# Layer 0 of a four-layer conditional residual network: four batches at once, as 2x2 blocks with seven block products in place of eight

## The chip, the cores and the metric

The kernel runs on one core of a Trainium2 chip. The time is the device time of one launch in microseconds. A core has TensorE (PE; its weight loads are shown as PEld), VectorE (DVE), ScalarE (ACT), GpSimd (POOL) and SyncE (SP, which only issues DMAs here). Each runs its own instructions in the order in which they were written, and waits on semaphores for the others.

## The reference

Activations x are 8 batches x 256 tokens x 1024 features. Each layer adds to x:

```
x = x + L0(x): x @ W0.T + 2 * lora, where logits = x @ Wr.T + 5 * onehot(lang[b]),
        the two best of 8 experts are gated by a softmax of their logits,
        h = x @ A[e].T (16 ranks for each expert), lora = (h * gate) @ B[e].T
x = x + L1(x): x @ W1.T + b1 + coeff[b] * (x @ (2 * mask[b] - 1))
x = x + L2(x): x @ w2[ids[b]].T           (1024 x 1024 weights, chosen for each batch)
x = x + L3(x): (x @ B3[ids[b]]) @ A3[ids[b]]   (rank 16)
```

W0 is the same for all batches; the weights of layers 1 and 2 differ from batch to batch.

## The kernel before

**Precision.** Every large product is split: each operand becomes a high half (a cast to fp32r, by ACT) and a low half (the source less the high half, by DVE), and TensorE adds hi·hi, hi·lo and lo·hi in PSUM. `three` (lines 408-423) does it with three 512-column matmuls for each k-block, 24 in all. `two` (425-439) has hi and lo of x side by side, 256 columns each, and needs eight matmuls of 512 and eight of 256 columns. The residual x + x @ W.T is had by adding the identity to W's diagonal block (`add_identity`, line 159) before it is split.

**Order.** The kernel works on pairs of batches q = 0..3 (512 tokens), one pair after another. `units` (lines 109-117) lists the work for a pair: "A" (the experts' first product, 24 matmuls), eight units of layer 0 (one for each block m of 128 output features, 24 matmuls each and three for the low-rank term, `lora`, line 451), sixteen of layer 1 and sixteen of layer 2 (m and batch j of the pair, each `two`). Layer 3 has rank 16 and is spread between other units (`proj`, `rank`, `fill`). `slot(i)` (line 656) writes all engines' work for unit i by hand: load the weights nine units ahead (`load`, SP's queue), `evacuate` the unit before out of PSUM (ACT copies one half, DVE adds the other), make high halves four units ahead (`prep_hi`, line 184) and low halves three ahead (`prep_lo`, 191), and then the matmuls (`main`). Layer 1's weights of a batch, mask times coefficient plus W1, are merged six or seven units ahead: `merge` (154, ACT) and `merge_add` (174, DVE).

**Router.** `logits` (259), transposes to token order (270), then some twenty small DVE operations and one exponential on ACT (`router`, lines 273-318) for the pair; `gate` (320) multiplies the experts' product by the gates and splits it, for `lora`.

**Buffers.** Ten 512 KB tiles for raw weights, five for high and four for low halves of weights, four x tiles of 2 MB, PSUM as two groups of four banks.

**Start.** `first_products` (486) interleaves the splits of x, of the experts' weights and of the first unit with their matmuls in pieces of 256 columns, as the first DMAs land.

Of the kernel before, what the change touches and what calls it, by code (L numbers as in the profile page):

```python
# [8 lines left out]
F32 = mybir.dt.float32  # L9
# [6 lines left out]
P = 128  # L16
NB = 8
T = 256
K = 8
E = 8  # L20
R = 16
LOAD_AHEAD = 9
PREP_AHEAD = 4
MERGE_AHEAD = (6, 7)
W1_BUFS = 3
RAW_BUFS = 10
# [6 lines left out]
def kernel(ctx: ExitStack, tc: tile.TileContext, x, lang, coeff, ids,  # L33
# [3 lines left out]

    nc = tc.nc
# [4 lines left out]
    hlp = ctx.enter_context(tc.tile_pool(name="hl", bufs=4))  # L43
    xp = ctx.enter_context(tc.tile_pool(name="xp", bufs=2))
    rawp = ctx.enter_context(tc.tile_pool(name="raw", bufs=RAW_BUFS))
    wp = ctx.enter_context(tc.tile_pool(name="w", bufs=4))
    l3p = ctx.enter_context(tc.tile_pool(name="l3", bufs=4))
    gp = ctx.enter_context(tc.tile_pool(name="g", bufs=1))
    ps = ctx.enter_context(tc.tile_pool(name="ps", bufs=4, space=PS))
    aux = ctx.enter_context(tc.tile_pool(name="aux", bufs=4, space=PS))  # L50

    D = PREP_AHEAD
    f32 = lambda ap: ap.bitcast(F32)


    xraw = {}

    def load_x(b, h, parts=1):

        t = rawp.tile([P, K // 2, T], F32, tag="raw", name=f"x{b}_{h}")  # L60
        n = K // 2 // parts
        for i in range(parts):
            c = slice(i * n, (i + 1) * n)
            nc.sync.dma_start(t[:, c, :], x[b, :, h * K // 2 + i * n:h * K // 2 + (i + 1) * n, :])
        xraw[b, h] = t
# [13 lines left out]
    for g in range(1, 4):  # L79
        nc.vector.tensor_tensor(sel, sel, ident[:, 32 * g:32 * g + R], ALU.add)  # L80
# [6 lines left out]


    def split(hi, lo, src):
        nc.scalar.copy(hi, src)  # L90
        return lambda: nc.vector.tensor_tensor(lo, src, f32(hi), ALU.subtract)

    x0 = {}

    def split_x(q):
        x0[q] = tuple(hlp.tile([P, K, 2 * T], FR, tag="hl", name=f"x0{h}{q}")
                      for h in ("hi", "lo"))

    def split_x_part(q, j, h, k0=0, k1=K // 2):
        hi, lo = x0[q]  # L100
        c = slice(j * T, (j + 1) * T)
        src = xraw[2 * q + j, h][:, k0:k1, :]
        k = slice(h * K // 2 + k0, h * K // 2 + k1)
        nc.scalar.copy(hi[:, k, c], src)
        return lambda: nc.vector.tensor_tensor(lo[:, k, c], src, f32(hi[:, k, c]),
                                               ALU.subtract)


    units = []
    for q in range(NB // 2):  # L110
        units.append(("A", q, 0, 0))
        units += [("L0", q, m, 0) for m in range(K)]
        units += [("L1", q, m, j) for m in range(K) for j in range(2)]
        order = [(m, j) for m in range(K) for j in range(2)]
        if q == NB // 2 - 1:
            order[-6:] = [(m, j) for j in range(2) for m in range(K - 3, K)]
        units += [("L2", q, m, j) for m, j in order]
    raws, ws, w1raw = {}, {}, {}

    def parts(i):  # L120

        n = 2 if i < 2 else 1
        return [slice(j * K // n, (j + 1) * K // n) for j in range(n)]

    def load(i):
        if i >= len(units):
            return
        kind, q, m, j = units[i]
        b = 2 * q + j
        if kind == "L1":  # L130
            if j == 0:
                w = rawp.tile([P, K, P], F32, tag="w1", name=f"w1_{q}_{m}", bufs=W1_BUFS)
                nc.sync.dma_start(w, w1[m])
                w1raw[q, m] = w
            t = rawp.tile([P, K, P], I32, tag="raw", name=f"raw{i}")
            nc.sync.dma_start(t, mask[b, m])
        else:
            t = rawp.tile([P, K, P], F32, tag="raw", name=f"raw{i}")
            if kind == "A":
                for c in parts(i):  # L140
                    nc.sync.dma_start(t[:, c], la[:, c])
            elif kind == "L0":
                for c in parts(i):
                    nc.sync.dma_start(t[:, c], w0[m][:, c])
            else:
                src = w2[bass.ds(adapter(b), 1), m]
                nc.sync.dma_start(t, src.rearrange("a p k c -> (a p) k c"))
        raws[i] = t


    def merge(i):
        if i < len(units) and units[i][0] == "L1":
            b = 2 * units[i][1] + units[i][3]
            nc.scalar.activation(f32(raws[i]), raws[i], AF.Identity,  # L154
                                 bias=negc[:, b:b + 1], scale=c2[:, b:b + 1])

    def add_identity(w, m):

        nc.vector.tensor_tensor(w[:, m, :], w[:, m, :], ident, ALU.add)  # L159

    folded = set()

    def fold(i):
        if i < len(units) and units[i][0] in ("L0", "L2") and i not in folded:
            add_identity(raws[i], units[i][2])
            folded.add(i)

    def merge_add(i):
        if i < len(units) and units[i][0] == "L1":
            s = f32(raws[i])  # L170
            _, q, m, j = units[i]
            if j == 0:
                add_identity(w1raw[q, m], m)
            nc.vector.tensor_tensor(s, s, w1raw[q, m], ALU.add)  # L174

    def source(i):
        return f32(raws[i]) if units[i][0] == "L1" else raws[i]

    def prep_hi(i):
        if i < len(units):  # L180
            fold(i)
            hi = wp.tile([P, K, P], FR, tag="whi", name=f"whi{i}", bufs=D + 1)
            for c in parts(i):
                nc.scalar.copy(hi[:, c], source(i)[:, c])  # L184
            ws[i] = hi

    def prep_lo(i):
        if i < len(units):
            lo = wp.tile([P, K, P], FR, tag="wlo", name=f"wlo{i}", bufs=D)
            for c in parts(i):  # L190
                nc.vector.tensor_tensor(lo[:, c], source(i)[:, c], f32(ws[i])[:, c],  # L191
                                        ALU.subtract)
            ws[i] = (ws[i], lo)
            raws.pop(i)
# [9 lines left out]
    nc.sync.dma_start(wrs, wr)  # L204
    load_x(0, 0, 2)
    load(0)
    load_x(0, 1, 2)
    load(1)
    load_x(1, 0, 2)
    load_x(1, 1, 2)  # L210
    lang_i = cst.tile([P, NB], I32, name="lang_i")
    nc.sync.dma_start(lang_i, lang.rearrange("(a b) -> a b", a=1).to_broadcast([P, NB]))
    c_sb = cst.tile([P, NB], F32, name="c_sb")
    nc.sync.dma_start(c_sb, coeff.rearrange("(a b) -> a b", a=1).to_broadcast([P, NB]))
    ids_raw = cst.tile([1, NB], I32, name="ids_raw")
    nc.sync.dma_start(ids_raw, ids.rearrange("(a b) -> a b", a=1))
    b1_sb = cst.tile([P, K], F32, name="b1_sb")
    nc.sync.dma_start(b1_sb, b1)

    load(2)  # L220
    lb_raw = rawp.tile([P, K * P], F32, tag="raw", name="lb_raw")
    nc.sync.dma_start(lb_raw, lb)

    bias = cst.tile([P, NB, E], F32, name="bias")
    c2 = cst.tile([P, NB], F32, name="c2")
    negc = cst.tile([P, NB], F32, name="negc")
    ids_sb = cst.tile([1, NB], I32, name="ids_sb")
    lbs = [cst.tile([P, K * P], FR, name=f"lb{n}") for n in range(2)]

    def constants():  # L230

        lang_f = cst.tile([P, NB], F32, name="lang_f")
        nc.vector.tensor_scalar(lang_f, lang_i, -1.0, float(E), ALU.mult, ALU.add)
        nc.vector.tensor_tensor(bias, rev.to_broadcast([P, NB, E]),
                                lang_f.rearrange("p (b o) -> p b o", o=1)
                                      .to_broadcast([P, NB, E]), ALU.is_equal)
        nc.vector.tensor_scalar(bias, bias, 5.0, None, ALU.mult)
        nc.vector.tensor_scalar(c2, c_sb, 2.0, None, ALU.mult)
        nc.vector.tensor_scalar(negc, c_sb, -1.0, None, ALU.mult)

        neg = cst.tile([1, NB], F32, name="neg")
        idf = cst.tile([1, NB], F32, name="idf")
        nc.vector.tensor_scalar(neg, ids_raw, 0.0, float(E), ALU.is_lt, ALU.mult)
        nc.vector.tensor_tensor(idf, ids_raw, neg, ALU.add)
        nc.vector.tensor_scalar(ids_sb, idf, 0.0, float(E - 1), ALU.max, ALU.min)


    NT = 4

    pls = {}  # L250

    def logits(b, h):


        q, j = divmod(b, 2)
        if (j, h) == (0, 0):
            pls[q] = aux.tile([P, 512], F32, tag="aux", name=f"pl{q}")
        for g in range(4):
            nc.tensor.matmul(pls[q][32 * g:32 * g + 32, j * T:(j + 1) * T],  # L259
                             wrs[:, 4 * h + g, :], xraw[b, h][:, g, :],  # L260
                             start=(h == 0), stop=(h == 1))
# [555 lines left out]
```

## Time and profile before

| what | value |
|---|---|
| median of 3 runs | 626.79 us (626.68 to 627.22) |
| profiled execution | 626.69 us, span 624.9 us |
| mean granted TensorE clock | 0.997 of full |
| PE / PEld / DVE / ACT / POOL busy | 99 / 84 / 74 / 58 / 0% of the span |
| DMA | 125.01 MB, 200 GB/s over the span |

The span goes from the first to the last instruction; the time has some 1.8 us around it. In a view of groups, a row has the line, engine, operation, output and inputs, shape and count, then busy time and the mean of one in ns, then the engine's idle time ahead of such instructions and who ended it. In a timeline, a row begins with the start and the duration in us. Durations of instructions that follow each other on an engine overlap, so their pace is read from one start to the next. The rows of tenths cut the span into 40 equal slices.

### The profile page before, as it was taken

Reading aid. Unit: us, or ns where it says so; the run is one execution under the profiler, and the core shown is the slowest. Engines: PE = TensorE matmul, PEld = TensorE weight load, DVE = VectorE, ACT = ScalarE, POOL = GpSimd, SP = SyncE. Lnnn points to the kernel's source line nnn. Section 1 sums busy time; section 2 is a strip of 40 time slices with the busy share of each in tenths; the row PEclk is TensorE's granted clock in tenths of the full one; section 3 lists DMA queues with packets and bytes.
Section 4 is the critical chain, followed back from the end, with each engine's and each line's share of the span. In section 5 each row is a group of like instructions: output and inputs, shape, how many; then the busy total and the mean of one; then the engine's idle time right before and its main releaser. Section 6 shows DMA issues by size and latency. Waiting matters only on the chain.

```text
span 624.9 us, 9250 instructions
## 1 busy us (share of the span) xinstructions
PE 616.8 (99%) x3458; PEld 522.9 (84%) x3458; DVE 460.8 (74%) x800; ACT 363.0 (58%) x552; POOL 1.0 (0%) x14
## 2 busy tenths in 40 slices
PE   8999999999999999999999999999999999999996
PEld 6888888888788888888878888888888888888885
DVE  6685898776657799778656689967765678987642
ACT  5375797564354498656335558865535446975421
POOL 0000000000000000000000000000000000000000
PEclk9999999999999999999999999999999999999998
DMA  8964575667725775475942778547684458755004
GB/s 279 400 213 162 201 269 174 201 210 278 252 68 169 230 273 195 143 246 190 345 140 76 203 238 278 179 142 249 197 315 135 130 174 270 246 191 170 34 0 136
DMA packets 38815, 125.01 MB, mean 200 GB/s; under 512 B 4722, under 2 KB 5874, under 8 KB 38770
## 3 DMA queue, kind: packets, MB, share of 16 engines
q1 hardware_dynamic: 38626, 124.15, 59.8%
q8 instruction: 27, 0.44, 0.3%
q10 hardware_dynamic: 144, 0.26, 0.1%
q14 instruction: 18, 0.15, 0.1%
HBM read 116.01 MB, written 8.39 MB: 199 GB/s over the span
## 4 chain that ended last, share of the span: by engine, by line
PE 98%; DMA 1%; SPq 0%; DVE 0%; ACT 0%; DVEq 0%; issue 0%
PE po L428 37%; PE po L436 20%; PE po L412 9%; PE po L420 9%; PE po L413 9%; PE po L454 1%; PE po L455 1%; PE po L456 1%; PE pl L259 1%; PE po L388 1%; PE pb L468 1%; PE ph L413 1%; PE ph L412 1%; PE ph L420 1%; DMA raw<-in_la 1%; PE ph L497 0%
## 5 line engine op out<-in xcount | busy, mean ns | idle before, releaser
L428 PE MATMUL po<-hl,whi 128*128 128x512 f32 x1016 | 254.5, 392 | 0.0
L428 PEld LDWEIGHTS po<-hl,whi 128*128 128x128 f32 x1016 | 182.9, 189 | 32.9
L191 DVE TENSOR_TENSOR wlo<-raw,whi 128x1024 fp32r<-128x1024 f32 (+1 forms) x166 | 199.1, 1205 | 2.1 <-ACT whi L184 2.1
L184 ACT CAST whi<-raw 128x1024 fp32r<-128x1024 f32 (+1 forms) x166 | 172.4, 1039 | 10.6 <-DVE raw L159 7.9
L436 PEld LDWEIGHTS po<-hl,wlo 128*128 128x128 f32 x1016 | 137.9, 190 | 11.3 <-DVE raw L159 1.2
L436 PE MATMUL po<-hl,wlo 128*128 128x256 f32 x1016 | 142.4, 283 | 0.0
L412 PE MATMUL po<-x0hi,whi 128*128 128x512 f32 x248 | 97.1, 392 | 0.0
L413 PE MATMUL po<-x0lo,whi 128*128 128x512 f32 x248 | 96.7, 390 | 0.0
L174 DVE TENSOR_TENSOR raw<-raw,w 128x1024 f32<-128x1024 f32 x64 | 78.1, 1221 | 3.6 <-ACT raw L154 2.6
L154 ACT ACTIVATE raw<-raw,negc,c 128x1024 f32<-128x1024 int32 x64 | 79.7, 1245 | 0.0
L717 ACT COPY xt<-po 128x256 f32<-128x256 f32 x63 | 23.4, 372 | 83.6 <-PE po L436 83.6
L420 PE MATMUL po<-x0hi,wlo 128*128 128x512 f32 x248 | 62.3, 393 | 0.0
L710 ACT CAST hl<-po 128x256 fp32r<-128x256 f32 x64 | 20.5, 377 | 71.6 <-PE po L456 71.4
L726 DVE TENSOR_TENSOR xt<-po,xt 128x256 f32<-128x256 f32 x63 | 26.7, 423 | 47.0 <-ACT xt L717 46.7
L724 DVE TENSOR_TENSOR hl<-po,hl 128x256 fp32r<-128x256 f32 x64 | 23.8, 420 | 46.1 <-ACT hl L710 40.7
L412 PEld LDWEIGHTS po<-x0hi,whi 128*128 128x128 f32 x248 | 46.5, 188 | 11.1 <-issue 1.2
L413 PEld LDWEIGHTS po<-x0lo,whi 128*128 128x128 f32 x248 | 46.6, 188 | 9.8
L420 PEld LDWEIGHTS po<-x0hi,wlo 128*128 128x128 f32 x248 | 45.4, 188 | 8.8
L720 ACT ACTIVATE sum<-po,b_sb 128x256 f32<-128x256 f32 x64 | 30.4, 475 | 23.4 <-PE po L436 23.1
L726 DVE TENSOR_TENSOR sum<-po,sum 128x256 f32<-128x256 f32 x64 | 26.9, 420 | 12.7 <-ACT sum L720 12.6
L724 DVE TENSOR_TENSOR hl<-sum,hl 128x256 fp32r<-128x256 f32 x64 | 26.9, 420 | 4.6 <-ACT hl L710 4.6
L710 ACT CAST hl<-sum 128x256 fp32r<-128x256 f32 x64 | 25.6, 400 | 7.6 <-DVE sum L726 7.6
(118 smaller groups left out, 378.8 us busy)
## 6 DMA issues: line engine op xcount, KB each, us to landing
raw<-in_w SPq DMA_DIRECT2D x95, 512.0 KB, 4.2
raw<-in_mask SPq DMA_DIRECT2D x64, 512.0 KB, 5.2
w<-in_w SPq DMA_DIRECT2D x32, 512.0 KB, 4.8
out<-xt SPq DMA_DIRECT2D x31, 256.0 KB, 3.1
x<-in_x SPq DMA_DIRECT2D x12, 512.0 KB, 4.6
a3raw<-in_a SPq DMA_DIRECT2D x8, 384.0 KB, 3.6
x<-in_x SPq DMA_DIRECT2D x8, 256.0 KB, 5.4
raw<-in_la SPq DMA_DIRECT2D x3, 512.0 KB, 3.4
```

The source lines that it names most:

```text
L154: nc.scalar.activation(f32(raws[i]), raws[i], AF.Identity, bias=negc[:, b:b + 1], scale=c2[:, b:b + 1])
L174: nc.vector.tensor_tensor(s, s, w1raw[q, m], ALU.add)
L184: nc.scalar.copy(hi[:, c], source(i)[:, c])
L191: nc.vector.tensor_tensor(lo[:, c], source(i)[:, c], f32(ws[i])[:, c], ALU.subtract)
L412: nc.tensor.matmul(po, hi[:, k, :], xhi[:, k, :], start=(k == 0), stop=False)
L413: nc.tensor.matmul(po, hi[:, k, :], xlo[:, k, :], start=False, stop=False)
L420: nc.tensor.matmul(po, lo[:, k, :], xhi[:, k, :], start=False, stop=(last and k == K - 1))
L428: nc.tensor.matmul(po, hi[:, k, :], xhl[:, k].rearrange("p h t -> p (h t)"), start=(k == 0), stop=False)
L436: nc.tensor.matmul(po[:, :T], lo[:, k, :], xhl[:, k, 0, :], start=False, stop=(k == K - 1))
L710: nc.scalar.copy(hi, p)
L724: nc.vector.tensor_tensor(lo, p, f32(hi), ALU.subtract)
L726: nc.vector.tensor_tensor(xs, p[:, :T], xs, ALU.add)
```

## The change

Layer 0 is done for four batches (a group g, two pairs p0 = 2g and p1 = 2g+1) at once. W0 is cut into 2x2 blocks A11..A22 of 512 output by 512 input features; x is cut into 2x2 blocks B11..B22 of 512 input features by one pair's 512 tokens. The 2x2 product is had by seven block products with sums and differences (S1..S4 of A, T1..T4 of B) in place of eight. Each block product is two slots of 24 matmuls (half of the inner dimension each, over four output blocks). A slot has two items of 512 KB to split: one of A or S, one of B or T. A group has 16 slots for layer 0: 14 for products, and slots 4 and 5, which make only the second pair's experts' product (12 matmuls each); the first pair's is beside slots 0 to 3 (6 matmuls each). Layers 1 and 2 then follow for each pair as before.

What moves with it:

- DVE makes S2, S3, T1, T2 and T3 from the raw blocks, in place (ten 1024-wide differences for a group). S1, S4 and T4 are made by DMAs from POOL's queue that add to a block in SBUF (`accum_op`), six for a group. Four merges of layer 1 in each group are also done by such a DMA.
- The sums of products are built in SBUF: ACT copies C11 and U2 out of PSUM, DVE adds into U2, U3, C21, C22 and C12 (ten 1024-wide additions), and `split_c` splits each pair's C for layer 1.
- The identity is added to diagonal blocks by POOL, not by DVE (`fold_block`).
- PSUM tiles are pairs of banks, two such tiles in rotation and four single banks. In layers 1 and 2 the two batches of an output block share one and are evacuated by one instruction (`joint`).
- x, the sums C, the split x of layer 1 and of layer 2 live in three 4 MB regions that are used in turn. Raw weights have nine tiles in place of ten, W1 two in place of three.
- Group 0's second router runs in slot 7 of layer 0; group 1's two routers run together at the end of layer 2 of pair 1.
- At the start, SP loads x and W0's first blocks in k-blocks, and the small constants after them.

The diff, cut to what carries this:

```diff
+    L0_PRODUCTS = [("A11", "B11"), ("A12", "B21"), None, ("S2", "T2"), ("S3", "T3"),
+                   ("A22", "T4"), ("S1", "T1"), ("S4", "B22")]
...
+    def merge_add(n):
...
+        if by_dma(q, m):
+            fold_block(s[:, m, :])
+            nc.gpsimd.dma_start(s, w1[m], accum_op=ALU.add)
+            return
...
+    def prep_lo(n):
+        if n not in los:
+            los[n] = wp.tile([P, 1024], FR, tag="wlo", name=f"wlo{n}", bufs=LO_AHEAD + 1)
+        return los[n]
...
+    def product(s, g, kks, start=False, lora=None, mid=()):
...
+        for m in range(4):
+            o = mms[g][m // 2][:, m % 2, :]
...
+            if m == 2:
+                for f in mid:
+                    f()
+            if lora:
+                lora(m, o)
+            for k in kks:
+                link(o, w[0][:, k, c], v[0][:, k], start=(start and k == 0), stop=False)
+                link(o, w[0][:, k, c], v[1][:, k], start=False, stop=False)
+            for k in kks:
+                link(o, w[1][:, k, c], v[0][:, k], start=False, stop=(k == 1))
...
+        o = 1 if g == 0 else 0
+        at(0 + o, *subs("S3", "A11", "A21", 0, 1), folds)
+        if g == 0:
+            at(1, constants)
+            at(3, lambda: router([p0]), lambda: expand(p0), lb_parts)
+            at(-5, lambda: gate(p0))
+            at(7, lambda: router([p1]), lambda: expand(p1))
+            at(10, lambda: gate(p1))
+        else:
+            at(-5, lambda: gate(p0))
+            at(2, lambda: expand(p0))
+            at(7, lambda: expand(p1))
+            at(8, lambda: gate(p1))
+        at(1 + o, lambda: s1_add(0), lambda: s1_add(1), *subs("T1", "B12", "B11", 0, 1))
+        at(2 + o, *subs("S2", "S3", "A22", 0), *subs("T2", "T1", "B22", 0))
+        at(3 + o, *subs("S2", "S3", "A22", 1), *subs("T2", "T1", "B22", 1))
+        at(5, lambda: t4_add(0))
+        at(6, lambda: t4_add(1), *subs("T3", "B22", "B12", 0, 1))
+        at(7, lambda: s4_add(0), lambda: s4_add(1))
+        for i, s in enumerate((7, 9, 13, 13)):
+            at(s, lambda i=i: split_c(p0, i))
...
+    def l0_evacuate(g, s):
+        for t in range(2):
...
+            if s == 2:
+                copy(c("U2"), m)
+            elif s == 6:
+                copy(c("C11"), m)
+            elif s == 8:
+                tt(c("U2"), m, c("U2"), ALU.add)
...
+    def l0_mids(g):
...
+            return {1: lambda: logits(p0), 2: lambda: by_token(p0), 3: lambda: logits(p1),
+                    4: lambda: [by_token(p1), gates_by_rank(p0)],
+                    8: lambda: gates_by_rank(p1)}
...
+    def l0_slot(n):
...
+        evacuate()
+        l0_evacuate(g, s)
+        if (g, s) == (0, 0):
+            head()
+        for work in w.get(-s, []) if s else []:
+            work()
+        highs(f + HI_AHEAD)
+        fold(f + HI_AHEAD + 1)
+        fold(f + HI_AHEAD + 2)
+        lows(f + LO_AHEAD)
+        for work in w.get(s, []):
+            work()
+        for u in merges.get(n, []):
+            merge_add(u)
+        if g == 0 and s == 0:
+            la_parts(0, 2, 4)
+        elif g == 0 and s == 1:
+            la_parts(0, 4, 8)
+        if (g, s) != (0, 0):
+            l0_main(g, s)
...
+    load_x(0, 0, 0, 1)
+    load_w0(0, "A11", 0, 2)
+    nc.sync.dma_start(LA[0][:, 0:2], la[:, 0:2])
+    load_x(0, 0, 1, 2)
+    load_x(0, 0, 2, 4)
+    load_w0(0, "A11", 1)
+    nc.sync.dma_start(LA[0][:, 2:4], la[:, 2:4])
+    load_x(0, 0, 4, 8)
+    load_constants()
+    load_w0(0, "A12", 0)
```

`HI_AHEAD` is 4 and `LO_AHEAD` is 3, in items; `lb_parts` splits the low-rank weights and their difference (three DVE subtractions of 1024 or 512 and one difference, two ACT copies); `at(-5, ...)` puts work ahead of slot 5's splits.

## The prediction

> **What bounds the kernel now.** I read the page first: the busy shares, then the chain of waits.
>
> ```profile
> PE 616.8 (99%) x3458; PEld 522.9 (84%) x3458; DVE 460.8 (74%) x800; ACT 363.0 (58%) x552; POOL 1.0 (0%) x14
> ...
> DVE  6685898776657799778656689967765678987642
> ...
> PEclk9999999999999999999999999999999999999998
> ...
> PE 98%; DMA 1%; SPq 0%; DVE 0%; ACT 0%; DVEq 0%; issue 0%
> ```
>
> TensorE is the chain: 98% of it, at full clock, with nothing between its matmuls. Whatever takes matmuls away shortens the kernel, so long as the other queues still deliver in time. The view of waits for PE has only 1.4 and 0.9 us, both before 8 us. DVE at 74% is the nearest other engine, and its slices are uneven: 9 in layer 1, 5 or 6 in layer 0.
>
> The groups by shape give the counts and durations of layer 0:
>
> ```profile
> L412 PE MATMUL po<-x0hi,whi 128*128 128x512 f32 x248 | 97.1, 392 | 0.0
> L413 PE MATMUL po<-x0lo,whi 128*128 128x512 f32 x248 | 96.7, 390 | 0.0
> L420 PE MATMUL po<-x0hi,wlo 128*128 128x512 f32 x248 | 62.3, 393 | 0.0
> ...
> L454 PE MATMUL po<-ghi,lb 128*128 128x512 f32 x32 | 12.7, 397 | 0.0
> L184 ACT CAST whi<-raw 128x1024 fp32r<-128x1024 f32 x162 | 170.1, 1050 | 9.2 <-DVE raw L159 6.9 <-issue 1.5 <-DVE raw L174 0.7
> ```
>
> The 390 ns of one matmul overlap with the next, so the timeline gives the pace:
>
> ```profile
> 35.93 0.39 PE L412 MATMUL po<-x0hi,whi 128*128 128x512 f32 x1
> ...
> 41.39 0.40 PE L454 MATMUL po<-ghi,lb 128*128 128x512 f32 x1
> ```
>
> One unit of 24 matmuls lasts 41.39 - 35.93 = 5.46 us, 0.2275 us each. DVE's timeline gives its pace in the same way:
>
> ```profile
> 129.12 1.22 DVE L105 TENSOR_TENSOR x0lo<-x,x0hi 128x1024 fp32r<-128x1024 f32 x1
> 130.25 1.22 DVE L191 TENSOR_TENSOR wlo<-raw,whi 128x1024 fp32r<-128x1024 f32 x1
> ...
> 21.18 0.29 DVE L276 TENSOR_REDUCE lv<-pt 128x32 f32<-128x128 f32 x1 [2.06 <-PE pt L270]
> ...
> 26.00 1.22 DVE L191 TENSOR_TENSOR wlo<-raw,whi 128x1024 fp32r<-128x1024 f32 x1
> ```
>
> A 1024-wide subtraction holds the queue for 1.14 us (a 512-wide one 0.61, by the same overlap). One router holds it from 21.18 to 26.00: 4.8 us, in some 20 small operations.
>
> **Matmuls removed.** Before, layer 0 has 8 units x 24 matmuls for each pair of batches: 768 in four pairs. After, each group of four batches has seven block products of two slots, 4 x 2 x 3 = 24 matmuls a slot: 7 x 2 x 24 x 2 groups = 672. The experts (96) and the low-rank term (96) keep their counts; so do layers 1 to 3, logits and transposes. Removed: 96 x 0.2275 = 21.8 us, all of it on the chain.
>
> **What DVE gets in layer 0.** For one group: 32 low halves where it had 18 for weights and 8 for x, ten block differences, ten sums out of PSUM, four splits of C. 56 x 1.14 = 64 us. With gates, merges and, in group 0, two routers and the lora weights it is some 86 us beside 102 us of matmuls. The mean fits. But the low halves have four buffers, two items a slot: DVE can't write those of slot s+1 before PE has left slot s-1. So work for slot s may spill only as far as PE's time in s and s+1. I walk through the slots where it is dense (PE time: product 5.46, experts of a slot 1.37, logits of a pair 1.9 to 2.1, four transposes 0.35).
>
> Group 0, slots 3 to 5. PE: slot 3 is 5.46 + 1.37 + 2.1 = 8.9, slot 4 has 12 matmuls and eight transposes, 3.4: together 12.3 us. DVE, from the start of slot 3: two lows 2.3, router with expand 4.8, lora weights 3.1 (1.14 + 2 x 0.61 and a wait of 0.7 for ACT's copy between them), S2 and T2 2.3, two lows for slot 5 2.3: 14.8 us. PE waits 2.5 us ahead of slot 5. Then S2/T2's other halves 2.3 and the gate 1.9 (two 0.61 and an ACT copy) end 4.2 us into slot 5, where the lora matmuls want the gate after 2.7: another 1.5 us.
>
> Group 0, slots 7 and 8. DVE: two lows 2.3, router 4.8, a split 1.1, then the first half of U2 1.1, which must empty the PSUM that slot 8's product starts in: 9.4 against PE's 5.46. 4.0 us. The later evacuations (slots 10, 12, 14, 16) find DVE with 3.5 to 4.6 us of work a slot: nothing.
>
> Group 1 has its router in layer 2, beside units of 2.79 us, as before. In its slot 7 the first split of C overwrites the buffer of the previous outputs, whose last store is issued at the start of that slot; the row of the stores says 3.1 us to landing. Copy, low half and U2 follow: about 6.5 against 5.46, 1.0 us.
>
> DVE's waits in sum: 2.5 + 1.5 + 4.0 + 1.0 = 9.0 us. Below: 0, if each wait finds slack that I don't see (the same router before made PE wait for nothing). Above: 14, with half a microsecond more for each of some ten handovers. I take 9.0, as each term is a count of known rows.
>
> **The start.** The view of stretches, with PE, PEld, DVE, ACT and POOL busy, clock, DMA share and GB/s:
>
> ```profile
> 0.00:8.00 8.00, 5.73 (x27) 4.45 (x28) 2.98 (x12) 3.28 (x5) 0.98 (x14) 1.00 0.73 204
> 8.00:16.00 8.00, 8.00 (x69) 6.72 (x70) 7.17 (x17) 4.95 (x9) 0.00 (x0) 1.00 1.02 355
> ...
> 68.00:113.00 45.00, 45.00 (x259) 39.58 (x258) 41.46 (x69) 37.93 (x58) 0.00 (x0) 1.00 0.62 211
> ```
>
> Before, PE reaches unit m=1 of layer 0 at 22.42 us, having done 48 matmuls (10.9), logits 1.9 and transposes 0.35: as if it had begun at 9.3. After, x's first k-block and half of A11 come first, and the product can begin at about 6.7 (first x landed at 5.48 here, issued 0.45 later). But ACT takes the high half of A12 before the expert weights of slot 1. A12 is behind some 4.06 MB; the first two rows give 1.63 MB by 8 us and 355 GB/s after, so it lands at about 15, and slot 1 starts near 16.2: 16.2 - 6.8 = 9.4. A loss of 0.1, between -2.6 (no such wait) and +1.5 (A12 lands 1.4 later).
>
> **What moves to POOL and its DMAs.** The 128 additions of the identity (L159, 285 ns on DVE) go to POOL, which has no two-input row; its 128x128 select took 294 ns. They are issued one or two slots ahead of their use, and DVE is freed of 36 us; layers 1 and 2 gain nothing, since PE never waited there. If POOL were slow, the merges of layer 1 would wait: with DVE at 41.5 of 45 us there (the third row), less the folds, there is room for 0.3 us each. Zero, with +2 above. Joint evacuations (512 wide for two of 256) only lighten ACT and DVE. PSUM in pairs leaves an evacuation one pair of units, 5.6 us, for 1.2 us on ACT and 1.3 on DVE: zero. Ten DMAs a group, 512 KB each, add into SBUF from POOL's queue; no row shows such a DMA. Plain ones land after 3.1 to 11.5 us (median 4.4). They have some four slots, 20 us, until their block is read: zero by either end.
>
> The Trainium skill speaks against the folds on POOL ("SBUF — State Buffer", Who interferes with whom): a DVE instruction with two SBUF inputs and a GpSimd instruction that reads SBUF shut each other out for a whole instruction. By its rule DVE would lose about what it is freed of, and the sum would stay, since I have counted nothing for that.
>
> A stall of 4.0 us is longer than any gap inside the trace, where the clock stands at 0.997. "TensorE: Matmul & The Clock Gate", Part 1, says that an idle window of 3.4 us halves TensorE's clock for about one more window; by the page that is an estimated 1.7 us more for one stall, and 615.7 for the sum. No row here shows it.
>
> **Sum.** Against the profiled execution, 626.69 us (span 624.9 and 1.8 around it; the median, 626.79, is 0.1 above): 626.7 - 21.8 + 9.0 + 0.1 = 614.0. Its own range, from the bounds above without all falling together: 608 to 620.
>
> **Rivals.**
> *DVE's spills are hidden.* Handovers overlap and the start gains: 626.7 - 21.8 + 2 = 607, down to 605 with the start's -2.6. For it: PE waited for no router before. Against: then DVE had only one item of 1.14 us per 5.46 us of matmuls in layer 0, now two and more.
> *The spills spread.* Every handover costs, POOL's folds delay DVE by as much again, the start loses: 614 + 5 + 2 + 1.5 to 4 = 622 to 625. For it: four buffers of low halves leave no reserve to work off a delay.
> *The adding DMAs are the bound (slower).* They stand in one queue, in order, from slot 2 to slot 12, and the folds of later units stand behind them. Ten in about 95 us leave 9.5 us each. If POOL takes them one after another and each needs t, PE loses 10 x (t - 9.5) a group: slower than before from t = 10.2; at 11.5 us, the longest landing of a plain load, 614 + 2 x 20 = 654. Against: plain loads of that size overlap in the trace and land at 4.4.
> *It saves less than it says.* Not possible by count: 96 rows of matmuls are gone from the program.
>
> **How the numbers follow.** Forecast 0.57, hidden spills 0.13, spreading spills 0.15, adding DMAs 0.14, and 0.01 for a chance balance. The range takes in the first three, 605 to 625, and leaves the fourth out. A measurement here can tell about 0.2% (1.25 us) from no change. Faster 0.84 (the first three, less a little of the third's end), same 0.02, slower 0.14.
>
> **What would show it.** Right: 864 matmuls of 512 columns in products, experts and lora where there were 960; PE's idle time in three places of the first group, ahead of slot 5 and inside it, and ahead of slot 8, each released by DVE; group 1 nearly free of them; PE still 97% of the chain; layers 1 and 2 at 2.79 us a unit. Wrong: PE waiting for a DMA or for POOL, idle time in layers 1 and 2, a granted clock below 0.98, or no wait at the routers.

## The result, and the profile after

The changed kernel takes 649.24 us (median of 4 runs, 647.77 to 650.81) against 626.79: a ratio of 1.036, interval 1.033 to 1.039. It is slower by 22 us; the prediction said 614.0, with 625 as its upper end.

The page of the kernel after (busy, tenths of the span, granted clock, chain):

```profile
PE 606.7 (93%) x3244; PEld 507.2 (78%) x3244; DVE 485.0 (75%) x563; ACT 370.1 (57%) x438; POOL 114.7 (18%) x156
...
PE   6998799999999899999999949999999989999985
...
PEclk9898799999999899999999989999999999999999
...
PE 33%; DVE 4%; issue 2%; DMA 1%; ACT 1%; ACTq 0%; SPq 0%
```

TensorE's row of nines has holes: at the start, in slices 4 and 5, at one place near 220 us, a deep one near 380 us, one near 530 us, and one in the tail. Below three of them the clock has an 8 or a 7, and behind the start an 8. The shares of the chain add up to 41% only, so nothing is read from them here.

The difference of the two spans, 649.0 - 624.9 = 24.1 us, comes apart with the first number alone. Before, PE was busy for 616.8 us and idle for 8.1. After, it is busy for 606.7 and idle for 42.3. The 96 matmuls less are worth 21.8 us, but busy time fell by 10.1 only: **11.7 us more for the same matmuls, and 34.2 us more of waiting.** -21.8 + 11.7 + 34.2 = 24.1. (PE has 214 instructions fewer, 3244 for 3458. The 118 beside the 96 are the same columns in wider pieces: 512 in place of 256 columns for the logits, the first units and a part of layer 3.)

Who ended the waits, from the view of waits for PE (sum, times, longest):

```profile
PE mm L587 <- DVE c L66: 12.1, 2, 8.4
PE po L519 <- DVE c L66: 7.8, 5, 2.3
PE ph L613 <- ACT laghi L641: 5.1, 1, 5.1
PE po L519 <- DVE sum L66: 4.4, 4, 1.1
PE mm L587 <- ACT ghi L398: 1.9, 1, 1.9
...
PE po L536 <- DVE c L66: 1.1, 1, 1.1
```

The first row is 3.71 us ahead of slot 8 of group 0 and 8.44 ahead of slot 8 of group 1. The third is the start, 12.67 to 17.80 us. The fifth is the gate inside slot 5. The second, fourth and sixth are in layers 1 and 2, where the prediction had nothing: ten gaps, 13.3 us together, one at the end of each of the first seven of the eight rounds of 16 units and three in the last units.

The 11.7 us of slower matmuls show in the view of stretches (PE, PEld, DVE, ACT, POOL busy, clock, DMA share, GB/s), here around the wait in group 1, which ends at 387.23:

```profile
379.00:384.00 5.00, 0.00 (x0) 0.00 (x0) 0.00 (x0) 0.35 (x1) 0.00 (x0) 1.00 0.86 249
384.00:387.00 3.00, 0.00 (x0) 0.00 (x0) 2.28 (x2) 3.00 (x4) 0.00 (x0) 0.50 0.00 0
387.00:391.00 4.00, 3.77 (x9) 3.03 (x10) 4.00 (x5) 0.06 (x1) 0.00 (x0) 0.52 0.15 38
391.00:395.00 4.00, 4.00 (x19) 3.29 (x19) 1.57 (x3) 2.52 (x3) 1.33 (x2) 1.00 0.24 97
```

From 387 to 391 PE is busy and does 9 matmuls; from 391 to 395 it does 19. The clock stays at half behind the wait. In the whole trace it does so behind the start, the gate, both waits ahead of slot 8, and one boundary. These five stretches cover 20.8 us in which PE works, which at half clock costs 10.4 us: nearly all of the 11.7.

### The profile page after: what moved, and what is told of

It reads as the page before. It is cut to its first block, busy times and chain, and to the rows that moved or that the text cites. A ratio compares the mean times of both kernels' runs of the same rounds, so it can differ in the third digit from the quotient of the medians.

```text
span 649.0 us, 8913 instructions
## 1 busy us (share of the span) xinstructions
PE 606.7 (93%) x3244; PEld 507.2 (78%) x3244; DVE 485.0 (75%) x563; ACT 370.1 (57%) x438; POOL 114.7 (18%) x156
## 3 DMA queue, kind: packets, MB, share of 16 engines
HBM read 114.96 MB, written 8.39 MB: 190 GB/s over the span
## 5 line engine op out<-in xcount | busy, mean ns | idle before, releaser
L66 DVE TENSOR_TENSOR wlo<-raw,whi 128x1024 fp32r<-128x1024 f32 x128 | 160.7, 1266 | 7.9 <-issue 7.9
L293 ACT CAST whi<-raw 128x1024 fp32r<-128x1024 f32 x128 | 133.7, 1048 | 22.3 <-issue 17.7
L587 PE MATMUL mm<-whi,whi 128*128 128x512 f32 x224 | 91.1, 407 | 12.1 <-DVE c L66 12.1
L587 PE MATMUL mm<-wlo,whi 128*128 128x512 f32 x224 | 90.0, 402 | 0.0
L236 POOL TENSOR_TENSOR raw<-raw,ident 128x128 f32<-128x128 f32 x72 | 52.0, 724 | 178.7 <-DMA raw<-in_w 100.0
L587 PE MATMUL mm<-whi,wlo 128*128 128x512 f32 x224 | 71.5, 398 | 0.0
L587 PEld LDWEIGHTS mm<-whi,whi 128*128 128x128 f32 x224 | 43.8, 196 | 24.6 <-ACT whi L293 8.8
L66 DVE TENSOR_TENSOR wlo<-x,whi 128x1024 fp32r<-128x1024 f32 (+1 forms) x37 | 44.3, 1207 | 11.1 <-ACT whi L293 6.8
L66 DVE TENSOR_TENSOR wlo<-A,whi 128x1024 fp32r<-128x1024 f32 (+1 forms) x29 | 34.9, 1203 | 21.8 <-PE mm L587 12.8
L587 PEld LDWEIGHTS mm<-whi,wlo 128*128 128x128 f32 x224 | 43.1, 192 | 9.9 <-DVE wlo L66 0.4
L587 PEld LDWEIGHTS mm<-wlo,whi 128*128 128x128 f32 x224 | 43.6, 195 | 9.1
```

The lines of the kernel that those rows point to most:

```text
L66: nc.vector.tensor_tensor(o, a, b, op)
L236: (eng or nc.gpsimd).tensor_tensor(t, t, ident, ALU.add)
L293: copy(prep_hi(i), flat(source(i)))
L587: mm(*args, skip_group_check=True, **kw)
```

## The experiments

The theory: four losses that have nothing to do with one another, each with a stretch of half clock behind it. Each of the first four kernels is meant to take one away.

**A PSUM bank for the boundary's second unit.**

```diff
+        if not joint and u % 2:
+            own = bank(3, f"po{n}")
...
+        elif u % 2:
+            po = own.rearrange("p (a n) -> p a n", a=1)
```

> The second unit of a pair that is not evacuated jointly (m=7 of every round of layers 1 and 2, and the last six units) gets a PSUM bank of its own in place of the second half of the pair's tile. Theory (a tile of two banks is released as one, so PE waits for the first unit's evacuation before the second unit's first matmul): the 14 gaps of 0.5 to 2.35 us at 171.9, 217.9, 266.7, 321.9, 374.6, 483.3, 529.4, 576.5, 617.0 us and in the tail, 13 us together, go, and little else changes: 649.2 - 13 = 636, between 634 and 639. Rival (the wait is for ACT and DVE being late at these places, whatever the bank): the gaps stay or move to the next unit, 647 to 650.

632.96 us (631.41 to 633.38): 16.3 less than after. All ten gaps, 13.3 us, are gone from the trace (the expectation counted some too many), and the half-clock stretch behind the one at 218 us with them: 220.2 to 223.6 us, 1.7 us of work. What is left, 1.3 us, is within the scatter of the runs. (Behind the gate's wait, 1.88 us here, the clock stayed full this time.) What they were, in the timeline of the kernel after (end of the first round of layer 1):

```profile
170.77 1.11 PE L528 MATMUL po<-hl,wlo 128*128 128x256 f32 x8
...
171.99 0.47 ACT L563 ACTIVATE sum<-po,b_sb 128x256 f32<-128x256 f32 x1 [0.65 <-PE po L528]
...
172.49 0.42 DVE L66 TENSOR_TENSOR sum<-po,sum 128x256 f32<-128x256 f32 x1 [0.15 <-ACT sum L563]
...
172.97 2.11 PE L519 MATMUL po<-hl,whi 128*128 128x512 f32 x8 [1.08 <-DVE sum L66]
```

At m = 7 the two batches are evacuated one by one (`joint` is false), but they still share a tile of two banks. The second batch's first matmul waits until ACT and DVE have emptied the first batch's half, though it writes the other bank. In layer 2 ACT's copy can stand behind its work on a mask that lands late, and 1.1 becomes 2.34 us:

```profile
218.26 1.24 ACT L258 ACTIVATE raw<-raw,negc,c 128x1024 f32<-128x1024 int32 x1 [1.54 <-DMA raw<-in_mask]
```

With a bank of its own the next unit follows without a gap:

```profile
168.57 1.12 PE L528 MATMUL po<-hl,wlo 128*128 128x256 f32 x8
169.52 2.00 PE L519 MATMUL po<-hl,whi 128*128 128x512 f32 x8
```

**The experts' weights of slot 1 first.**

```diff
             experts(0, 0, 1, k, k)
+        la_parts(0, 2, 4)
...
-        if g == 0 and s == 0:
-            la_parts(0, 2, 4)
```

> The experts' weights of slot 1 are split on ACT and DVE straight after the first product, ahead of A12's high half in ACT's queue. Theory (the first gap, 5.1 us at 12.7, is ACT standing behind A12's load): PE goes on with the experts and the rest of slot 0's work, then waits for A12 itself; the gap shrinks to 3 to 4 us and the half clock after it stays partly: 649.2 - 2 = 647, between 644 and 649. Rival (the gap is only ACT's order, A12 itself being in time): the gap goes with the slow clock behind it, 649.2 - 5 - 2.5 = 641.5.

644.81 us (642.68 to 645.05): 4.4 less. By its time that is inside the theory's range and not as low as the rival's 641.5, but the trace has the rival's cause. ACT's timeline in this kernel:

```profile
11.55 0.41 ACT L641 CAST laghi<-c 128x256 fp32r<-128x256 f32 x1 [2.79 <-DMA c<-in_la]
...
15.84 1.06 ACT L293 CAST whi<-A 128x1024 fp32r<-128x1024 f32 x1 [1.70 <-DMA A<-in_w]
```

ACT still waits for A12 (its cast starts at 15.84, at 16.39 in the kernel after), but TensorE no longer does: A12's first use is two slots on. The gap of 5.13 us becomes two of 0.72 and 0.95. From 13 to 26 us the mean clock is 1.00, where it was 0.74.

**S4's adding DMAs two slots later in group 1.**

```diff
-        at(7, lambda: s4_add(0), lambda: s4_add(1))
+        at(9 if g else 7, lambda: s4_add(0), lambda: s4_add(1))
```

> In group 1 the two adding DMAs for S4 are issued in slot 9 in place of slot 7. Theory (three adding DMAs at once hold up the stores whose buffer the first split of C overwrites): the stores land after some 4 us again, the wait of 8.4 us ahead of slot 8 becomes 1 to 2 us, and the half clock after it, some 3 us, goes too: 649.2 - 7 - 3 = 639, between 637 and 643. Rival A (the wait is DVE's chain of copy, low half and U2, as the prediction counted, with the stores a bystander): 8.4 stays, 649. Rival B (S4 is late now and slot 12 or 13 waits for it): a gap of 5 us or more there, 644 to 649.

648.42 us (647.86 to 651.87), no change, the gap 8.39 us. This tells nothing of the theory, because the edit moved nothing in time. POOL's timeline here:

```profile
367.82 1.21 POOL L679 DMA_DIRECT2D A<-in_w  x1
369.67 0.87 POOL L679 DMA_DIRECT2D A<-in_w  x1 [0.63 <-DMA out<-c]
```

The two are issued in slot 7 as they were. POOL has nothing between these and the slots before, so the place in the program is no time on an idle queue; only a wait for data is.

**Group 0's routers spread.** Low-rank weights in slot 2 and their difference in slot 9, the second halves of S2 and T2 behind the first gate, and:

```diff
-            at(7, lambda: router([p1]), lambda: expand(p1))
-            at(10, lambda: gate(p1))
+            at(11, lambda: router([p1]), lambda: expand(p1))
+            at(-13, lambda: gate(p1))
```

> In group 0 DVE's dense stretches are spread: the low-rank weights are split in slot 2 and their difference in slot 9, the second halves of S2 and T2 come behind the first gate, the second router moves from slot 7 to slot 11, its gate to slot 13 and the low-rank matmuls of slot 13 behind its products. Theory (PE waits for DVE's queue at slots 5 and 8, 6.2 us, and runs at half clock behind these gaps for some 4 us): 649.2 - 6 - 4 = 639, between 637 and 643. Rival (DVE is full over the whole of layer 0, so that the wait only moves): one gap of 3 to 6 us at slot 6 or at 11 to 14, 645 to 650.

641.29 us (638.79 to 642.52): 8.0 less. The gaps at slot 5 are gone, the one ahead of slot 8 is 1.31 us in place of 3.71, and no new one over 0.4 us came in layer 0 of group 0.

**The wait in group 1, from both ends.** ACT's and DVE's timelines of the kernel after, and, as the last row, the first matmul of slot 8:

```profile
383.64 1.04 ACT L660 CAST hl<-c 128x1024 fp32r<-128x1024 f32 x1 [10.12 <-issue]
...
384.72 1.22 DVE L66 TENSOR_TENSOR hl<-c,hl 128x1024 fp32r<-128x1024 f32 x1 [9.45 <-ACT hl L660]
...
385.87 2.35 DVE L66 TENSOR_TENSOR c<-mm,c 128x1024 f32<-128x1024 f32 x2
...
387.23 0.77 PE L587 MATMUL mm<-whi,whi 128*128 128x512 f32 x1 [8.44 <-DVE c L66]
```

ACT waits 10.1 us before it may write hl, DVE waits for ACT, and the evacuation of U2 that PE wants stands behind both. The view of the tile `out` says what ACT waited for:

```profile
  ACT hl L660: 10.1, 1
...
DMA to landing us min/median/max: 2.5/2.8/10.6
```

The last stores out of the buffer that hl takes over land after 10.6 us, where the median is 2.8; three adding DMAs, issued from 369.6 to 372.1 us, are in flight beside them. Two kernels take the chain apart. The first leaves the stores as they are and moves the split behind the evacuation:

```diff
-        for i, s in enumerate((7, 9, 13, 13)):
+        for i, s in enumerate((8 if g else 7, 9, 13, 13)):
```

> In group 1 the first split of C stands in slot 8, behind the evacuation that empties PSUM, in place of slot 7, ahead of it. ACT's copy still waits for the last stores. Theory (PE's 8.4 us ahead of slot 8 are that split waiting for the stores at the head of the queues that also evacuate): the gap becomes 0.5 us or nothing, and the half clock behind it, some 3 us, goes: 649.2 - 8.4 - 3 = 638, between 636 and 641. Rival (ACT and DVE, held by the stores a slot later, then leave slots 9 and 10 without high and low halves): a gap of 3 to 6 us moves there, 643 to 648.

640.88 us (639.65 to 643.47): 8.4 less. The gap ahead of slot 8 is gone, and 3.55 us stand ahead of slot 10. The rival had a gap of that size there, but from missing halves; this one ends with DVE's evacuation. The second split, still ahead of it, has become late through the first. The other kernel leaves the order and holds the adding DMAs back by data:

```diff
+            nc.gpsimd.tensor_tensor(t, u2, ident, ALU.add)
...
+            at(8, hold, lambda: s4_add(0), lambda: s4_add(1))
```

> In group 1 a 128x128 addition on POOL that reads U2 as slot 8's evacuation leaves it stands ahead of the two adding DMAs for S4, so that they can't be issued before the split of C. (The kernel that only wrote them two slots later had POOL issue them at 367.8 and 369.7 us of its span all the same: that queue had nothing to wait for.) Theory (the three adding DMAs hold up the last stores, 2.8 us to landing for the others and 10.6 for these): the stores land after 4 us or less, the split begins some 6 us earlier, the gap ahead of slot 8 becomes 1 to 3 us: 649.2 - 6.5 - 2.5 = 640, between 638 and 643. Rival (these stores are slow by themselves, or the one adding DMA for T4 is enough): 10 us to landing, gap 7 us or more, 647 to 650.

642.2 us (641.56 to 645.47): 7.0 less: the time is within the theory's range, the gap of 3.32 us and the stores at 6.3 us are a little over what it said:

```profile
DMA to landing us min/median/max: 2.5/2.7/6.3
```

So two of the three adding DMAs were worth 4.3 of the 7.8 us that the slowest store was late. The other kernels bear it out: with three at once the slowest store takes 10.3 to 12.8 us in all nine profiles, with two held back 6.3 here and 6.4 in the last kernel below. The T4 addition and the mask loads stay beside it; which of them holds the other 3.5 us was not tried, nor whether plain DMAs of that size in place of the adding ones would do the same.

**The identity additions on DVE again.** One word in `fold_block` (`nc.vector`).

> Every identity addition goes back from POOL to DVE. Theory (they cost PE nothing on POOL; on DVE they are 0.285 us each, some 120 of them, 34 us, of which only those in the dense slots of group 0 show): PE's waits at the routers grow by 1 to 2 us, 649.2 + 1.5 = 651, between 649 and 653. Rival (POOL and DVE hold each other up, so that DVE's subtractions shorten and the layer-0 waits with them): 645 to 647.5.

652.35 us (649.1 to 654.07), 3.1 more by the medians; the intervals of the ratios to before overlap (1.035 to 1.041 here), so a loss is likely and a gain doesn't show. DVE's work of other kinds does become shorter, above all its largest group, 1266 ns a piece in the kernel after:

```profile
L66 DVE TENSOR_TENSOR wlo<-raw,whi 128x1024 fp32r<-128x1024 f32 x128 | 155.0, 1218 | 7.2 <-issue 6.6 <-PE po L528 0.4
```

122 additions of 0.285 us are 34.8 us, but DVE's busy time grew by 14.1 only, from 485.0 to 499.1. So up to 20.7 us of busy time had gone to the neighbour on POOL; part of that is overlap, as additions that follow each other closely share some of their time (in the kernel before, one of 0.28 us at 131.38 is followed by the next at 131.58). The largest group alone shows 5.7 us (160.7 against 155.0). "SBUF — State Buffer", Who interferes with whom, in the Trainium skill, says that such instructions shut each other out whole. The traces agree in kind: POOL's addition takes 0.45 us at the least and up to 1.46 in the group of raw tiles of the kernel after, up to 2.9 in that of the `w` tiles. That DVE loses "about what it is freed of", as the prediction read the page, is more than the busy times allow: 20.7 of 34.8 us at most.

**The price of the half clock alone.** 32 matmuls on data that lie ready, ahead of slot 8's product in group 1, into a bank that nobody reads.

> 32 more matmuls of 512 columns, of data that lie ready, into a PSUM bank that nobody reads, stand on PE's queue ahead of slot 8's product in group 1, where PE waits for 8.4 us. They are 7.3 us of work and end before that wait does. Theory (behind a gap of this length PE runs at half clock for a while, which costs 3 us here beside the gap): the stretches after it stand at a clock of 0.99 or more and the time is 649.2 - 3 = 646, between 645 and 647.5. Rival (the low clock costs nothing, as other engines or DMAs set the pace there): 649.0 to 650.

647.2 us (644.39 to 648.26): 2.0 less. In the stretches of this kernel the clock does not fall:

```profile
387.00:391.00 4.00, 4.00 (x20) 3.29 (x19) 3.31 (x5) 0.75 (x2) 0.00 (x0) 1.00 0.35 106
```

20 matmuls where there were 9. The direction is the theory's; its 3 us were too many. In the kernel after, the clock is half until 390.8 us and the wait ends at 387.2: 3.6 us of work, worth 1.8. The profiled run is no clean price either: its last stores landed after 12.6 us in place of 10.6, and PE got from slot 7 to slot 8 in 10.4 us (375.85 to 386.27) in place of 8.4.

**All together.** First the edits of four kernels (bank, experts' weights, routers, the first split in slot 8), then the same with S4 held back and, in both groups, the first two splits in slots 8 and 10.

> The edits of four kernels in one: a PSUM bank of its own for the second unit at the boundaries, the experts' weights of slot 1 first, group 0's routers spread, and in group 1 the first split of C a slot later. Theory (the four losses are separate and add up with the half clocks behind them): 649.2 - 16.3 - 4.4 - 8.0 - 8.4 = 612, between 609 and 615, and PE's work is then shown to be worth the 21.8 us of the prediction less what is left of its waits. Rival (the waits share a cause, such as DVE or the DMA engines being full, and come back elsewhere): 617 to 627.

613.78 us (611.77 to 615.48), ratio to before 0.977, interval 0.975 to 0.980. The four sum to 37.1 and gave 35.5: the losses were separate, and nothing of size came back elsewhere. The two largest gaps left are the ones named for the next kernel, 3.27 and 1.32 us; the others are under 1 us, but for 1.4 at the very start.

> The same, with S4's adding DMAs of group 1 held back behind U2, and in both groups the first two splits of C in slots 8 and 10, behind the evacuations that empty PSUM, in place of ahead of them. Theory (a gap of 3.5 us is left ahead of slot 10 of group 1, where the split, late through the stores, stands ahead of the evacuation on DVE, and 1.3 us ahead of slot 8 of group 0): both go, with a window of half clock: 612 - 3.5 - 1.3 - 1.5 = 606, between 604 and 609. Rival (S4, held back, comes late for slot 14, or the splits for layer 1): a new gap of 2 us or more at slots 12 to 16, 609 to 614.

608.32 us (607.92 to 609.43), ratio 0.970, interval 0.968 to 0.972: 18.5 us faster than before and 40.9 faster than after. Both gaps are gone, and no late S4 took their place. Its page:

```profile
PE 595.4 (98%) x3244; PEld 501.0 (83%) x3244; DVE 485.9 (80%) x563; ACT 370.7 (61%) x438; POOL 121.6 (20%) x157
...
PEclk9999999999999999999999999999999999999999
```

The same 3244 matmuls take 595.4 us of PE, where 616.8 - 21.8 = 595.0 was to be expected. Behind the first 1.4 us, PE's four gaps over 0.4 us sum to 2.8.

## Why the prediction was wrong

**The saving was right.** 96 matmuls at 0.2275 us: the last kernel shows it to 0.4 us of busy time, and its 608.3 us are 3.3 above 626.8 - 21.8 = 605.0. The 864 matmuls are there (672, 96 and 96). That the agreement is as close as 0.4 us is in part luck: "logits ... keep their counts" holds for the columns only, and their busy time went from 9.1 to 7.5 us.

**The router terms had the right places and the right order of work.** "2.5 + 1.5 + 4.0" for group 0 stands against gaps of 0.54 + 1.92 + 3.71 us, 6.2 for 8.0. DVE ended the first and the third, the ACT copy within the gate the second. Taking them away gave 8.0 us, the sum of the prediction, but by chance: 4.8 are gaps (the 1.31 us stayed) and the rest the clock behind them, which that sum didn't hold.

**The step that failed first: "PSUM in pairs leaves an evacuation one pair of units ... zero".** It holds for the units evacuated jointly. I costed the pairs by the common case and did not walk the units where `joint` is false, those of m = 7 and the last six. Measured: 16.3 us, the largest term. This alone puts the sum at 630, above before.

**Group 1's slot 7: "the row of the stores says 3.1 us to landing".** The mechanism, the split of C that waits for the previous outputs, is the one that happened. The term of 1.0 us was sized with a duration from a trace in which no adding DMA ran. With three of them the landing took 10.6, the wait 8.4 us, and the two kernels that cut the chain gave 8.4 and 7.0. The same oversight stands in "They have some four slots ... zero by either end": I asked when the adding DMAs would be done, and not whom they would hold up. The rival that made them the bound, to which all of the chance of a slower kernel was given, was wrong in its mechanism. They overlapped in flight and landed after 6.4 to 8.6 us by their medians, below its 10.2 (the two for S4 in group 1 after 10.4), and none of PE's waits ended with one of their blocks.

**The start: a loss of 0.1, at most 1.5.** The edit that takes most of the wait away gave 4.4 us. The order in ACT's queue was read rightly; A12 landed at 16.4 for 15, and slot 1 began at 17.8 for 16.2, 1.6 late, just over the bound. The rest is likely the clock behind the wait, and the gain of 2.6 that the sum had listed as its lower bound and not taken; the 4.4 were not taken apart further.

**The clock, left out of the sum.** The prediction gave a page's estimate of 1.7 us for one stall and did not count it. The busy times say 606.7 - 595.4 = 11.3 us for the whole kernel. The Trainium skill ("TensorE: Matmul & The Clock Gate", Part 1) speaks of a free-running window of 3.4 us, and the half-clock stretches of the kernel after last 3.4 us or twice that (56.3 to 59.7, 73.4 to 80.2, 384.0 to 390.8 us), which agrees. Its condition, an idle window, does not tell these waits apart: in the kernel after, the gate's wait of 1.92 us and a boundary's 2.34, both shorter than a window, were followed by a slow stretch; in the kernel with S4 held back, a wait of 3.32 us was not. Of what the prediction named as signs that it was wrong, two came: idle time in layers 1 and 2, and a mean clock below 0.98 (0.977).

In sum the six edits gave 16.3 + 4.4 + 8.0 + 8.4 one by one and 5.5 for the last two together, 42.6 us, and 40.9 in one kernel.

## What to carry to other kernels

When a step changes how a buffer is shared, walk its exceptions (first, last, odd units), not its common case: a wait of 1 us that comes at every boundary outweighs a large one that comes once. When a kernel at full TensorE occupation gets holes, price each hole with the slow matmuls behind it, by busy time per matmul. And moving an instruction in the program moves it in time only if its queue is busy or it waits for data.

## What the runs showed of the hardware

- Half-clock stretches came behind waits of 1.9 us and more, but not behind each: 3.32 us left none. The gate's wait stands in eight traces at 1.88 to 1.92 us. In three of them (the kernel after, the experts' weights first, the split in slot 8) a slow stretch follows, and PE does 15 matmuls in the 5.6 us behind it; in the other five the clock stays full, and it does 22. In the three, the wait begins within 0.5 us of a multiple of 3.41 us (the length of the shortest stretch) from the clock's other changes; in the five, 0.8 to 1.4 us ahead of one. By these eight traces the phase of the wait counts, and not its length alone.
- The kernel after scatters by 0.5% from run to run (647.77 to 650.81). The kernel before did so by 0.1% beside it, and by 0.4% over all of its runs (626.48 to 628.82). That the phase makes the difference is likely, and was not tried.
- Plain stores of 256 KB that land in 2.8 us took 10.3 to 12.8, the slowest of them, beside three adding DMAs of 512 KB, and 6.3 or 6.4 beside one.
- A 128x128 addition took POOL 0.45 to 0.51 us (once 0.77) where no addition or subtraction of DVE ran at the same time, and up to 2.9 us in the group of `w` tiles, against 0.285 us on DVE. POOL's durations are rough in such a profile.
